# A state-space and spiking feed-forward block: a new order of work at the head, other buffers for the sums of the last two tiles, and a last piece of 224 columns

## The chip, the cores and the metric

The kernel runs on one core of a Trainium2 chip. The core has a matrix engine (TensorE, PE in the profile; its weight loads are listed apart as PEld), a vector engine (VectorE, DVE), an engine for pointwise functions (ScalarE, ACT), GpSimd (POOL) and SyncE (SP), which here only issues the transfers between the device's memory and the core. Each engine works through its own list of instructions in order, and semaphores make it wait for the others. The metric is the device time of one execution in microseconds; of several runs the median is taken.

## The reference

Sixteen sequences of 1024 tokens with 256 features pass two layers, each behind a normalisation whose shift, scale and gate come from a condition vector c:

```python
mod = (_silu(L0_c) @ L0_wmod).reshape(L0_c.shape[0], 6, 1, -1)
sa, ca, ga, sb, cb, gb = (mod[:, 0], ..., mod[:, 5])
ga = (2 * (ga >= 0) - 1) * jnp.maximum(jnp.abs(ga), 0.25)     # gb alike
h = _layernorm(x) * (1 + ca) + sa
x = x + ga * state_space(h)
h = _layernorm(x) * (1 + cb) + sb
x = x + gb * feed_forward(h)
```

The state-space layer computes `Bu = (h @ W_B.T + b_B) * dt`, runs the recurrence `state = A_bar * state + Bu` over the 1024 tokens, with `A_bar = exp(-exp(log_A) * dt)`, and gives `state @ W_C.T + b_C + h @ W_D.T + b_D`. The feed-forward layer squares the positive part of `h @ W_fc.T` (1024 values per token), multiplies by `W_proj.T`, and counts how often a leaky neuron with this input fires in five steps; the count is divided by 5. All of it is in float32.

## The kernel before

**Tiles and stages.** The tokens are cut into 32 tiles of 512, two to a sequence. A tile passes these stages: statistics and normalisation with tokens on the partitions (`moments`, `aggregate`, `root`, `newton_v`, `normalise_by`), a turn to features on the partitions, the product with W_B (`state_input`, tile pb), the bias (`state_bias`), the recurrence (`state_scan`), the two products with W_D and W_C into one sum (`mix_h`, `mix_xs`, tile py), the gated residual (`mix_out`), a turn back, second statistics, a second turn, the expansion (`expand`, tile pf, in four pairs of blocks), its squares (hid), the contraction (`contract`, tile pp, summed over the four pairs), and the neuron (`spike`, line 532). `spike` needs no loop over time: the count is the number of five thresholds that the input exceeds, so it is one compare and four compare-and-adds on DVE, read from the sum. `gated` (ACT) and `output` (POOL and a store, or DVE at the very end) finish a tile.

**Three passes for float32.** Every product is made of halves: a high part that the fast matrix format holds exactly, and the rest, the low part. `PASSES` (line 228) lists (weight half, data half): high with high, low with high, high with low. One 128-row block of 512 columns therefore takes six products. ACT writes a high part (`scaled_hi`, `state_hi`, `S.activation(wb[:, 0], ...)`), DVE the low part (`scaled_lo`, `state_lo`, `halves_lo`, `hidden_lo`).

**Who sets the order.** Nothing is planned by costs: all engines are wrapped in `InOrder` (line 71), so each one executes its instructions in the order in which the program text issues them. What a line waits for is then only data and buffers. The sums lie in three groups of buffers of 512 float32 columns: `ps_f` (four), `ps_y` (two, for the state-space mix) and `ps_p` (two, for the contraction).

**The head, lines 125 to 152 and 604 to 701.** SP issues the loads in text order: cols (c, log_A, biases and log_dt, 20 KB), the first tile xq_0 in two halves, then pieces of `wmod` (wm1), W_B (fb), W_D (fd), W_C (fcm) and so on. `run_idle(n)` issues n products of a zero tile with itself; nothing reads their result. `silu_c` computes SiLU of c: exponentials on ACT, then add, reciprocal and product on DVE. `decay_steps` is a generator of 20 small DVE steps, each dependent on the one before, that gives A_bar; `decay(n)` issues the next n of them, and lines in between use it to fill DVE. `columns(wm, which, name)` computes one 256-wide part of `mod` as columns: eight products 16 columns wide (ps_ca, ps_sa, ps_ga, and ps_cb, ps_sb, ps_gb later). `ps_bb` and `ps_bd`, also 16 wide, carry the shift sa through W_B and W_D. Tiles 0 and 1 are turned on PE (`transpose`, and `transpose_back` into pm); from tile 2 on that goes over memory (`hop`).

Before the change, twelve zero products open the program and two groups of three more stand behind ps_ca and ps_sa. DVE finishes SiLU ahead of the first statistics. The statistics of tile 1 are put between the two scans of tile 0 and behind them (lines 648 and 669).

**The tail, lines 556 to 587 and 956 to 991.** `period_before_last(30)` and `last_tile(31)`. Tile 30's contraction takes the two `ps_p` buffers, which tile 29's spikes read until then. In the last tile the 256 output features are two blocks m of 128: m = 0 is summed over all 512 columns in a `ps_y` buffer, m = 1 in two pieces of 256 columns in the `ps_p` buffers, each piece followed by its spike and its store.

## Time and profile before

| what | value |
|---|---|
| median of 3 runs | 992.76 us (991.89 to 993.47) |
| profiled execution, its own time | 991.63 us |
| its span, first to last instruction | 989.8 us |
| PE busy | 981.9 us, 99% of the span |
| DVE busy | 851.1 us, 86% |
| ACT busy | 767.1 us, 77% |
| POOL busy | 284.5 us, 29% |
| mean granted clock of TensorE | 0.999 |

The page lists an engine's busy time, the chain of work that ended last (followed back from the last instruction to whatever released each step), and groups of alike instructions. Nearly all instructions stand at line 81, the helper that issues in order, so one goes by the tile names: `py<-xsp,wc` is a product that reads xsp and wc and writes py. A row of the chain or of the timeline gives the start in us from the beginning of the span, the duration, the engine and what was done, and, in brackets, how long the engine had been idle and what ended that. In a table of stretches each engine has its busy us and, in brackets, its instructions; the granted clock of TensorE (1.00 is full), the share of the transfer engines and GB/s follow. Rows of one engine can overlap by some 0.1 us, since an instruction begins while the one before it drains.

### The profile page before, as it was taken

How to read it: one execution, taken by the hardware profiler on the slowest of the kernel's cores; microseconds unless marked ns; L12 is line 12 of the kernel's file. 1: busy time of each engine (PE TensorE's matmuls, PEld its weight loads, DVE VectorE, ACT ScalarE, POOL GpSimd, SP SyncE). 2: the span in 40 equal slices, each digit the busy share in tenths (PEclk: the TensorE clock that was granted, in tenths of full speed). 3: DMA queues.
4: the chain of work that ended last, by engine and by line, in shares of the span. 5: the costliest groups of instructions: out<-in, count | busy, mean ns of one | idle time of the engine just before them, and what ended most of it. 6: DMA issues, size and time to landing. Idle time of an engine off the chain costs nothing.

```text
span 989.8 us, 13366 instructions
## 1 busy us (share of the span) xinstructions
PE 981.9 (99%) x4410; PEld 813.8 (82%) x4410; DVE 851.1 (86%) x1618; ACT 767.1 (77%) x1142; POOL 284.5 (29%) x313
## 2 busy tenths in 40 slices
PE   9999999999999999999999999999999999999997
PEld 8888788888888888888888888888888888888886
DVE  8789998888988889888889888889888889887777
ACT  6786887787877887877877877877877878777784
POOL 0002243223233223233133333133332233331122
PEclk9999999999999999999999999999999999999999
DMA  8224555455454455554455454554554554443321
GB/s 312 83 82 153 179 182 149 149 171 168 153 170 137 152 179 153 157 171 133 154 179 158 155 172 127 169 170 152 168 152 146 170 167 153 149 139 128 96 86 43
DMA packets 125350, 150.07 MB, mean 152 GB/s; under 512 B 9568, under 2 KB 89184, under 8 KB 125280
## 3 DMA queue, kind: packets, MB, share of 16 engines
q1 hardware_dynamic: 125280, 149.22, 48.1%
q8 instruction: 34, 0.56, 0.2%
q14 instruction: 36, 0.29, 0.1%
HBM read 85.22 MB, written 63.96 MB: 151 GB/s over the span
## 4 chain that ended last, share of the span: by engine, by line
PE 91%; DVE 5%; ACT 2%; issue 1%; DMA 0%; SPq 0%; DVEq 0%
PE pf L81 33%; PE pp L81 32%; PE py L81 16%; PE pb L81 8%; DVE o L81 2%; PE ps_zero L81 1%; ACT a L81 1%; ACT xn_a L81 1%; ACT hid L81 0%; DMA hop_x<-w_x 0%; DVE h_b L81 0%; DVE st_b L81 0%; DVE x L81 0%; DVE h_a L81 0%; DVE e_b L81 0%
## 5 line engine op out<-in xcount | busy, mean ns | idle before, releaser
L81 PE MATMUL pp<-hid,wp 128*128 128x512 f32 (+1 forms) x1560 | 365.4, 387 | 0.4 <-DVE o L81 0.4
L81 PE MATMUL pf<-h_b,wf 128*128 128x512 f32 x1536 | 363.9, 390 | 0.0
L81 PEld LDWEIGHTS pp<-hid,wp 128*128 128x128 f32 x1560 | 289.2, 188 | 61.4 <-DVE hid L81 1.5
L81 PEld LDWEIGHTS pf<-h_b,wf 128*128 128x128 f32 x1536 | 288.1, 188 | 59.8
L81 ACT ACTIVATE a<-pf,bias_f 128x512 f32<-128x512 f32 x256 | 167.0, 680 | 157.1 <-PE pf L81 157.0
L81 DVE TENSOR_TENSOR hid<-a,hid 128x1024 fp32r<-128x1024 f32 x127 | 152.8, 1223 | 89.2 <-ACT hid L81 89.2
L81 POOL TENSOR_TENSOR o<-o,x 128x512 f32<-128x512 f32 x64 | 110.0, 1739 | 296.0 <-ACT o L81 296.0
L81 DVE SCALAR_TENSOR_TENSOR o<-pp,o 128x512 f32<-128x512 f32 (+1 forms) x260 | 177.5, 683 | 8.0
L81 ACT ACTIVATE hid<-a 128x1024 fp32r<-128x1024 f32 x128 | 135.9, 1061 | 4.0
L81 ACT ACTIVATE a<-a 128x1024 f32<-128x1024 f32 x128 | 135.8, 1061 | 3.9
L81 POOL TENSOR_SCALAR x<-x,gac 128x512 f32<-128x512 f32 x58 | 90.2, 1564 | 51.8 <-DVE o L81 51.8
L81 POOL TENSOR_SCALAR v_a<-mv_a 128x4 f32<-128x4 f32 x26 | 15.6, 600 | 278.0 <-DVE mv_a L81 278.0
L81 PE MATMUL py<-xsp,wc 128*128 128x512 f32 x384 | 92.7, 390 | 0.0
L81 PE MATMUL pb<-h_a,wb 128*128 128x512 f32 x384 | 92.6, 390 | 0.0
L81 PE MATMUL py<-h_a,wd 128*128 128x512 f32 x384 | 92.2, 389 | 0.0
L81 PEld LDWEIGHTS py<-h_a,wd 128*128 128x128 f32 x384 | 72.1, 188 | 14.9
L81 PEld LDWEIGHTS pb<-h_a,wb 128*128 128x128 f32 x384 | 71.9, 188 | 15.0
L81 PEld LDWEIGHTS py<-xsp,wc 128*128 128x128 f32 x384 | 71.8, 188 | 15.0 <-DVE xsp L81 0.3
L81 ACT ACTIVATE xn_a<-xq,m_a,r_a 128x256 f32<-128x256 f32 x123 | 63.8, 592 | 3.2 <-DVE m_a L81 3.2
L81 ACT ACTIVATE xn_b<-xm,m_b,r_b 128x256 f32<-128x256 f32 x120 | 62.0, 588 | 4.0 <-DVE m_b L81 4.0
L81 DVE TENSOR_SCALAR o<-pp 128x512 f32<-128x512 f32 (+1 forms) x65 | 43.4, 668 | 14.1 <-PE pp L81 14.1
L81 ACT ACTIVATE o<-o,gb 128x512 f32<-128x512 f32 x64 | 42.3, 709 | 6.2 <-issue 4.7
(124 smaller groups left out, 835.6 us busy)
## 6 DMA issues: line engine op xcount, KB each, us to landing
x<-in_x SPq DMA_DIRECT2D x32, 512.0 KB, 5.1
out<-o SPq DMA_DIRECT2D x63, 256.0 KB, 6.9
xq<-in_xq SPq DMA_DIRECT2D x31, 512.0 KB, 6.7
hop_a<-w_a SPq DMA_DIRECT2D x120, 128.0 KB, 2.2
v_a<-hop_a SPq DMA_DIRECT2D x30, 512.0 KB, 4.0
hop_x<-w_x SPq DMA_DIRECT2D x120, 128.0 KB, 3.1
xm<-hop_x SPq DMA_DIRECT2D x30, 512.0 KB, 3.2
hop_b<-w_b SPq DMA_DIRECT2D x120, 128.0 KB, 2.2
```

Of the source, the lines that this page charges most:

```text
L81: return self.tc.keep_in_program_order(issue(*args, **kwargs))
```

## The change

In the head:

- SP issues the first half of xq_0, then cols, then the second half.
- The three DVE steps of SiLU move from `silu_c` into the front of `decay_steps` (23 steps now), so they are issued between the first statistics; these come right behind the zero products in the text, and ps_ca behind them. The two groups of three zero products go; the twelve at the start stay.
- The first normalisation gives three of four blocks to DVE. ACT's high part of W_B, s1 and the low part of W_B come behind it; ps_sa comes behind the transposes of a0; the remaining decay steps are spread anew, one behind each low part of h_a0 and six behind both.
- `state_input(0)` is issued in two parts, with ps_bb between them. The low part of W_D moves behind the first scan, and `mix_h(0)` takes its passes in the order high-high, high-low, low-high.
- All four statistics of tile 1 move behind tile 0's scans and the low parts of the states and of W_C. Its normalisation is split S, V, S, V. ps_cb and ps_sb come ahead of the transposes of a1.

In the tail:

- Tile 30's contraction is summed in the `ps_y` buffers. The low part of its first pair of hid is issued ahead of tile 29's second spike.
- In the last tile block m = 0 and the first piece of m = 1 are summed in `ps_p`, the last piece in `ps_y`; the pieces have 288 and 224 columns.

```diff
     col = const.tile([P, KD * NB + 4 * KD + 1], F32, name="col")
-    Q.dma_start(out=col, in_=cols)
     xqs[0] = io.tile([P, SUB, D], F32, tag="xq", name="xq_0", bufs=2)
     for s in (slice(0, 2), slice(2, 4)):
         Q.dma_start(out=xqs[0][:, s], in_=xq[0][:, s])
+        if s.start == 0:
+            Q.dma_start(out=col, in_=cols)
...
-        V.tensor_scalar(sil, sil, 1.0, None, ALU.add)
-        V.reciprocal(sil, sil)
-        V.tensor_tensor(sil, sil, cs, ALU.mult)
     def decay_steps():
+        yield V.tensor_scalar(sil, sil, 1.0, None, ALU.add)
+        yield V.reciprocal(sil, sil)
+        yield V.tensor_tensor(sil, sil, cs, ALU.mult)
...
-    def scaled_lo(key, src):
+    def scaled_lo(key, src, between=lambda: None):
...
+            between()
...
-    def mix_part(t, w, v, first, last):
-        for passes in (PASSES[:2], PASSES[2:]):
+    def mix_part(t, w, v, first, last, order=PASSES):
+        for passes in (order[:2], order[2:]):
...
                 if (t, m) not in accs:
-                    accs[t, m] = ps_p.tile([P, TT], F32, tag="ps_p", name=f"pp_{t}_{m}")
+                    pool, tag = (ps_y, "ps_y") if t == TILES - 2 else (ps_p, "ps_p")
+                    accs[t, m] = pool.tile([P, TT], F32, tag=tag, name=f"pp_{t}_{m}")
...
-        half = TT // 2
+        cut = TT // 2 + 32
...
-        late = [ps_y.tile([P, TT], F32, tag="ps_y", name=f"pp_{t}_0")]
-        late += [ps_p.tile([P, half], F32, tag="ps_p", name=f"pp_{t}_1_{g}") for g in range(2)]
-        for acc, m, cols in zip(late, (0, 1, 1), (slice(0, TT), slice(0, half), slice(half, TT))):
+        for m, cols in ((0, slice(0, TT)), (1, slice(0, cut)), (1, slice(cut, TT))):
             at = m, cols.start
+            pool, tag = (ps_y, "ps_y") if cols.start else (ps_p, "ps_p")
+            acc = pool.tile([P, cols.stop - cols.start], F32, tag=tag, name=f"pp_{t}_{m}_{cols.start}")
...
+    moments("a0", blocks_of(xqs[0]), between=lambda: decay(1))
     ps_ca = columns(wm1, 1, "ca")
-    run_idle(3)
-    ps_sa = columns(wm1, 0, "sa")
-    run_idle(3)
-    decay(3)
-    moments("a0", blocks_of(xqs[0]), between=lambda: decay(1))
     aggregate("a0")
     root("a0")
+    newton_v("a0", lambda: decay(1))
+    normalise_by("a0", blocks_of(xqs[0]), (V, S, V, V))
     S.activation(wb[:, 0], fb, AF.Identity, scale=edt)
-    newton_v("a0", lambda: decay(1))
-    normalise_by("a0", blocks_of(xqs[0]), (V, S, V, S))
+    V.tensor_scalar(s1, ps_ca, 1.0, None, ALU.add)
+    decay(2)
+    V.scalar_tensor_tensor(wb[:, 1], fb, edt, wb[:, 0].bitcast(F32), ALU.mult, ALU.subtract)
+    decay(1)
+    transpose("a0")
+    ps_sa = columns(wm1, 0, "sa")
+    scaled_hi("a0", lambda k: pts["a0", k])
+    scaled_lo("a0", lambda k: pts["a0", k], lambda: decay(1))
     S.activation(sa, ps_sa, AF.Copy)
-    V.tensor_scalar(s1, ps_ca, 1.0, None, ALU.add)
-    V.scalar_tensor_tensor(wb[:, 1], fb, edt, wb[:, 0].bitcast(F32), ALU.mult, ALU.subtract)
-    transpose("a0")
-    decay(5)
+    decay(6)
+    S.activation(wd[:, 0], fd, AF.Copy)
+    S.activation(wc[:, 0], fcm, AF.Copy)
+    state_input(0, (0,))
...
-    scaled_hi("a0", lambda k: pts["a0", k])
-    scaled_lo("a0", lambda k: pts["a0", k])
-    S.activation(wd[:, 0], fd, AF.Copy)
+    state_input(0, (1,))
...
     decay(8)
-    V.tensor_tensor(wd[:, 1], fd, wd[:, 0].bitcast(F32), ALU.subtract)
-    S.activation(wc[:, 0], fcm, AF.Copy)
-    state_input(0)
     state_bias(0)
     state_scan(0, (0,))
-    moments("a1", blocks_of(xqs[1]), blocks=(0, 1))
-    mix_h(0)
+    V.tensor_tensor(wd[:, 1], fd, wd[:, 0].bitcast(F32), ALU.subtract)
+    mix_h(0, (PASSES[0], PASSES[2], PASSES[1]))
...
     state_scan(0, (1,))
-    moments("a1", blocks_of(xqs[1]), blocks=(2, 3))
+    state_hi(0, slice(1, 2))
+    state_lo(0, slice(0, 1))
+    V.tensor_tensor(wc[:, 1], fcm, wc[:, 0].bitcast(F32), ALU.subtract)
+    state_lo(0, slice(1, 2))
+    moments("a1", blocks_of(xqs[1]))
     aggregate("a1")
     root("a1")
-    state_hi(0, slice(1, 2))
-    V.tensor_tensor(wc[:, 1], fcm, wc[:, 0].bitcast(F32), ALU.subtract)
-    state_lo(0, slice(0, 1))
     gates = shift_gate()
     newton_v("a1", lambda: next(gates, None))
-    state_lo(0, slice(1, 2))
     for _ in gates:
         pass
-    normalise_by("a1", blocks_of(xqs[1]), (S, S, V, S))
+    normalise_by("a1", blocks_of(xqs[1]), (S, V, S, V))
     mix_xs(0)
-    transpose("a1")
     ps_cb = columns(wm2, 1, "cb")
     ps_sb = columns(wm2, 0, "sb")
+    transpose("a1")
...
         expand(t, 1)
+        hidden_lo(t, 0)
         spike(t - 1, accs.pop((t - 1, 1)), (1, 0))
-        hidden_lo(t, 0)
```

More of the change, by code (lines that the diff above doesn't have):

```diff
@@ L411, in adaln_kernel, with state_input @@
     pbs = {}
-    def state_input(t):
+    def state_input(t, blocks=range(KD)):
         h = hs[f"a{t}"]
-        for m in range(KD):
+        for m in blocks:
             ps = pbs[t, m] = ps_f.tile([P, TT], F32, tag="ps_f", name=f"pb_{t}_{m}")
@@ L448, in mix_part, with mix_h @@
                          first and passes[0] == PASSES[0], last and passes[0] != PASSES[0], True, passes, True)
-    def mix_h(t):
+    def mix_h(t, order=PASSES):
         for m in range(KD):
             ys[t, m] = ps_y.tile([P, TT], F32, tag="ps_y", name=f"py_{t}_{m}")
-        mix_part(t, wd, hs[f"a{t}"], True, False)
+        mix_part(t, wd, hs[f"a{t}"], True, False, order)
     def mix_xs(t):
```

## The prediction

> **What bounds the kernel now.** I read the page first (busy shares, then the chain that ended last), then that chain in order of time at both ends of the span, then the rows of the vector engine (DVE) and of ScalarE (ACT) for the first 40 us, then a table of stretches for the granted clock. The page says who holds the end:

> ```profile
> span 989.8 us, 13366 instructions
> PE 981.9 (99%) x4410; PEld 813.8 (82%) x4410; DVE 851.1 (86%) x1618; ACT 767.1 (77%) x1142; POOL 284.5 (29%) x313
> ...
> PE 91%; DVE 5%; ACT 2%; issue 1%; DMA 0%; SPq 0%; DVEq 0%
> ```

> TensorE (PE) is the bound nearly everywhere; between 118 and 978 us it runs from one product to the next, and no edit touches that stretch except the last two tiles. So the change is decided at its two ends. The chain in order of time, at the head:

> ```profile
> 1.47 4.47 PE ps_zero L81 x12
> 5.93 0.92 PE ps_ca L81 x8
> 6.85 0.79 PE ps_zero L81 x3
> 7.64 0.80 PE ps_sa L81 x8
> 8.44 0.80 PE ps_zero L81 x3
> 9.24 0.87 PE pt_a L81 x8
> 10.11 0.80 PE ps_bb L81 x8
> 10.91 2.92 PE pb L81 x12
> ...
> 23.78 0.92 PE pm L81 x8
> 24.70 2.77 PE pb L81 x12
> ...
> 39.27 0.02 issue
> 39.30 0.02 ACT sil L81
> ```

> PE holds the head without a gap up to 39.3 us, the two groups of three zero products among its work; then ACT and DVE hold the chain until 118. A head that ends later or earlier on PE at 39.3 moves everything behind it by as much. What DVE does meanwhile:

> ```profile
> 14.57 0.73 DVE L81 BATCH_NORM_STATS2 st_a<-xq 128x6 f32<-128x256 f32 x2
> ...
> 21.92 1.36 DVE L81 TENSOR_TENSOR x<-x,x 128x512 f32<-128x512 f32 x2 [0.96 <-ACT x L81]
> ```

> Here the reader is to see how near DVE is to the bound: tile 1's statistics lie between the scans, and the two adds that PE's transposes pm wait for come 0.96 us after DVE ran out of work. The tail, from the same chain:

> ```profile
> 950.29 8.39 PE pp L81 x36
> 958.68 5.44 PE pf L81 x24
> ...
> 978.10 0.70 DVE o L81
> ...
> 986.14 0.48 DVE o L81
> ```

> 36 products at the steady 2.72 us per 12 are 8.16; tile 30's first sums take 8.39, so 0.23 us are waits. From 978.1 DVE holds the end.

> **The change part by part: the head.** All times are in the profiled execution's span. A row's mean overlaps the next row by some 0.08 us, so I add the distances between starts.

> Loads: the first half of xq_0 goes from second to first place on SP's queue, cols from first to second. Before, they were issued at 0.72 (cols) and 1.15 and landed 1.8 and 2.6 us later, at 2.5 and 3.75. The half issued at 0.72 lands at 3.3; cols, issued at 1.2 behind it, between 3.0 (its own 1.8) and 3.75 (the 2.6 of the row before it); I take 3.15. The second half landed at 4.5 and has the same bytes ahead of it: 4.25 to 4.5. Nothing behind them moves, and the weights of ps_ca land at 5.7 as before.

> First statistics: four BATCH_NORM_STATS2 with one step after each were 4.02 to 5.61. Now they start at 3.3, the steps between them are SiLU's (its reciprocal 0.35, the rest 0.1 each), and the third waits for the second half: aggregates end at 5.7 (5.98 before). Root and Newton take 1.33 as before: m_a at 7.03. ACT's wb no longer lies before its xn block. DVE now does three of the four blocks, 3 x 0.33 from 7.06: xn complete at 8.13 (8.43 before, with PE taking it only at 9.08). So PE idles from 6.8 to about 8.2, the six zero products (1.59 us of chain) shrink to this gap, and the transposes end at 8.95 instead of 10.11.

> PE then does ps_sa (0.9), the six products of pb's block 0 from 9.6 (1.4, with DVE's second low part, 10.0 to 10.75, just in time), ps_bb until 12.0, block 1 until 13.4. At pb PE is 1.16 ahead.

> DVE does not keep that lead. Behind the second low part (start 10.0) come seven dependent steps of the decay, 0.19 each, until 12.0, when ps_bb is ready too; two bias_b (0.20 each), four more steps (0.75): scan 0 starts at 13.2, against 13.44. From there I add DVE's own distances in the new order: scan 1.13, wd low 0.61, scan 1.13, xsp low 0.60, wc low 0.58, xsp low 0.60, four statistics 1.29, aggregates 0.36, ACT's root with its two handovers 0.36, Newton with four gate steps 1.16: m_a at 21.0, against 19.6. The statistics, which lay in the shade of the scans, and wd low are now in this row of work. ACT's two blocks of xn, 1.03 with the handover, and its first x, 0.80, follow; then the two adds 0.66 and 0.69, and the last four transposes of pm 0.42. That is 13.2 + 11.42: tile 1's pb starts at 24.62 instead of 24.46, **0.16 later**. PE is not short of other work before that: mix_h ends at 16.1 (its low weights are ready at 15.0, and the new order wants them last), mix_xs at 20.7, ps_cb, ps_sb and the transposes of a1 at 23.3; then it waits for the adds. ACT's scaled_hi of a1 stays behind its x and in front of pb. So the lead of 1.16 is gone at pm, where a wait for DVE stands in place of the zero products.

> Later in the head: DVE starts tile 0's second statistics 0.9 later (after the low part of h_a1), the root 0.5 later, and xn_b is complete at 30.2 where PE wants it at 30.2. No further loss. load_q(2) waits for xn_a0 and leaves 0.3 earlier, load_q(3) for xn_a1 and load(2) for the adds, each 0.9 later; xq_3 is read at 49, x_2 at 37. They cost nothing as long as they land in the 6 to 7 us of their rows.

> **The tail.** Tile 30's sums take the two buffers that tile 31's mix left at 929.7, so PE no longer waits for tile 29's second spike (950.85), and the low part of hid 30,0, now ahead of that spike, is ready at 948.5 instead of 951.98. Both waits go: **-0.23**. The spike ends 1.1 later, at 952; its gating on ACT comes at 956.9. The last tile's sums go where tile 29's and tile 30's first spikes have long released. DVE's row from 966 to 978 starts with PE's end of tile 30, so it moves with it; the 0.3 that PE waits for tile 31's low parts stays.

> The last pieces: from 512 and 256 columns DVE's distance is 0.725 and 0.459, so 288 costs 0.492, 224 costs 0.425. Five each: the sum over both pieces is the same, and both start when DVE is free (PE ends the 224 piece 0.3 before). Only the final operation on 224 columns saves 0.03, its store of 112 KB perhaps 0.04: **-0.07**.

> Sum: 989.8 + 0.16 - 0.23 - 0.07 = 989.66, and 1.83 around the span as in the profiled execution (991.63): 991.5. That execution lies 1.13 under the median of 992.76, which gives 992.6 by medians. One thing speaks for somewhat less: before, PE has no slack from 1.47 to 9.24, so any delay of the cold first products reaches the end, and the runs differ by 1.84 us (991.63 to 993.47) for a reason that this trace does not show; the new gap of 1.4 us at 6.8 would swallow such a delay. At nothing to half of the 1.13, I take 0.3: **992.3**.

> [...] Granted clock first. The twelve cold zero products took 4.47 us where twelve of pf take 2.88, so a cold spell costs 1.6. In a stretch with only narrow products and transposes the clock stayed full:

> ```profile
> 21.05:24.45 3.40, 3.40 (x33) 3.40 (x32) 2.53 (x5) 2.84 (x6) 0.00 (x0) 1.00 0.59 188
> ```

> By that row, narrow work is enough, and the price of removing the zero products is nothing. [...] I go by the row, which has no idle time in it, though; that difference is a rival.

> **The rivals.** (1) Slower, by the clock: without zero products PE has no 512-column work from 5.93 to 9.6 and idles 1.4 of that. If the clock falls there, pb and the first mix run cold: 1.6, or 3.2 if the spell is twice as long, so 994 to 995.6. It is slower than 0.2% (2 us) from about ten to twelve cold products on. Against it: the row above. Chance 0.15. (2) Faster: DVE's row is shorter than I add, and PE keeps its 1.16: 992.76 - 1.16 - 0.30 = 991.3; with a delay of the first products also swallowed, down to 990.2. It needs DVE to make 1.3 us less between 13.2 and 23.5, and DVE's rows there have no idle time to lose. Chance 0.22. (3) The tail's 0.23 stays, because the product waits for something else than the spike and hid: 992.6, inside my forecast. The forecast (0.63, own range 991.6 to 993.2) takes the landings of xq_0 and cols from 0.1 early to 0.3 late, and 0.3 on DVE's row.

> **How the numbers follow.** 0.2% is about 2 us, what a measurement of this kernel can tell from no change: under 990.8 or over 994.75. Half of rival 2 lies under 990.8, with a little of the forecast: 0.13. Of rival 1, some two thirds lie over 994.75 when both spells count and the median is hit: 0.10. The rest, 0.77, is within. The range 990.4 to 994.5 leaves out about one in ten on each side.

> **What the next profile would show.** Right: ps_ca followed by a gap of some 1.4 us on PE; pb of tile 0 near 9.6; scan 0 near 13.2; pm waiting for DVE x, and tile 1's pb at 24.6; tile 30's first 36 pp in 8.16; pieces of 288 and 224 with DVE last. Wrong: a granted clock under 1.00 or 512-column products 0.4 apart after 6 us (rival 1); pm following the transposes of a1 without a wait (rival 2); a wait of pp for hid or o at 950 (rival 3). A second wait on PE between 25 and 39, where I found room of 0.1 to 0.3 only (xn_b), would make it slower than I say.

## The result and the profile after

The changed kernel takes 995.78 us (median of 17 runs, 991.92 to 998.49) against 992.62 us for the kernel before (17 runs, 991.75 to 993.47): ratio 1.0024, interval 1.0015 to 1.0033. It is slower by 0.24% (the ratio is taken over all runs; between the medians the difference is 3.2 us, 0.32%), and its runs form two groups: six of 991.9 to 992.8 us whose mean granted clock is 0.998 or 0.999, and eleven of 994.7 to 998.5 us with a clock of 0.992 to 0.997. Below, a run with 0.997 or less is said to have fallen. Two executions far outside all others, 1094.32 us of e5 and 2022.04 us of the kernel before in the same comparison, are left out of the figures. The profiled execution is one of the second group (997.29 us). From its page, the span, the busy times and the granted clock in 40 slices:

```profile
span 995.5 us, 13352 instructions
PE 986.3 (99%) x4404; PEld 817.9 (82%) x4404; DVE 852.0 (86%) x1620; ACT 766.1 (77%) x1140; POOL 284.6 (29%) x313
...
PEclk7999999999999999999999999999999999999999
```

Six products fewer, and PE is busy 4.4 us longer. The clock is low in the first slice only. The chain in order of time, at the head:

```profile
1.62 4.36 DMA xq<-in_xq
...
9.20 1.32 PE pt_a L81 x8
10.52 1.39 PE ps_sa L81 x8
11.91 2.75 PE pb L81 x6
14.65 1.52 PE ps_bb L81 x8
16.18 2.75 PE pb L81 x6
18.92 3.68 PE py L81 x12
...
30.62 2.85 PE pb L81 x12
```

Six products of pb take 2.75 us; in the kernel before twelve took 2.92. Tile 1's pb starts at 30.62, against 24.70 before. A table of stretches (busy us of PE, PEld, DVE, ACT and POOL with their instructions, then TensorE's granted clock) shows why:

```profile
7.12:10.53 3.41, 2.23 (x19) 1.98 (x18) 2.97 (x19) 1.92 (x4) 0.00 (x0) 1.00 1.03 385
10.53:13.95 3.42, 3.42 (x13) 3.02 (x13) 2.81 (x12) 2.09 (x5) 0.00 (x0) 0.50 1.03 420
13.95:17.36 3.41, 3.41 (x13) 3.03 (x12) 1.04 (x6) 0.69 (x1) 0.00 (x0) 0.50 1.02 420
17.36:20.77 3.41, 3.41 (x9) 2.64 (x8) 2.91 (x4) 1.21 (x2) 0.00 (x0) 0.50 1.04 386
20.77:24.20 3.43, 3.43 (x25) 3.07 (x23) 3.43 (x12) 0.64 (x1) 0.00 (x0) 1.00 0.13 42
```

The clock is halved from 10.53 to 20.77 us, three times 3.41 us; in e9, below, it is halved once for as long (10.79 to 14.20). Stretches of this length, counted from where the clock became full, are called steps here. In the step before the fall (7.12 to 10.53) PE was busy 2.23 us, with ps_ca, the transposes and nothing 512 columns wide. This is the first rival of the prediction. The tail, from the chain, and the row of DVE that begins the last piece, from the timeline:

```profile
955.99 8.16 PE pp L81 x36
964.15 5.44 PE pf L81 x24
```

```profile
989.77 0.39 DVE L81 TENSOR_SCALAR o<-pp 128x224 f32<-128x224 f32 x1 [0.28 <-issue]
```

Tile 30's first 36 products take 8.16, so the two waits there are gone, as predicted. Ahead of the piece of 224 columns DVE stands still for 0.28 us for nothing that the profile shows.

### The profile page after: what moved, and what is told of

The parts are those of the page before. It is cut to its first block, busy times and chain, and to the rows that moved or that the text cites. A ratio compares the mean times of both kernels' runs of the same rounds, so it can differ in the third digit from the quotient of the medians.

```text
span 995.5 us, 13352 instructions
## 1 busy us (share of the span) xinstructions
PE 986.3 (99%) x4404; PEld 817.9 (82%) x4404; DVE 852.0 (86%) x1620; ACT 766.1 (77%) x1140; POOL 284.6 (29%) x313
## 4 chain that ended last, share of the span: by engine, by line
PE 90%; DVE 5%; ACT 2%; DMA 1%; issue 1%; SPq 0%; DVEq 0%
PE pf L81 33%; PE pp L81 32%; PE py L81 16%; PE pb L81 8%; DVE o L81 2%; ACT a L81 1%; ACT xn_a L81 0%; DMA xq<-in_xq 0%; ACT hid L81 0%; DMA hop_x<-w_x 0%; DVE h_b L81 0%; DVE st_b L81 0%; DVE x L81 0%; DVE h_a L81 0%; DVE w_x L81 0%
## 5 line engine op out<-in xcount | busy, mean ns | idle before, releaser
L81 PE MATMUL pp<-hid,wp 128*128 128x512 f32 (+2 forms) x1560 | 365.1, 386 | 0.4 <-DVE o L81 0.4
L81 PE MATMUL pf<-h_b,wf 128*128 128x512 f32 x1536 | 363.9, 390 | 0.0
L81 PEld LDWEIGHTS pp<-hid,wp 128*128 128x128 f32 x1560 | 289.5, 188 | 60.6 <-DVE hid L81 1.2
L81 PEld LDWEIGHTS pf<-h_b,wf 128*128 128x128 f32 x1536 | 288.2, 188 | 59.7
L81 ACT ACTIVATE a<-pf,bias_f 128x512 f32<-128x512 f32 x256 | 167.0, 680 | 156.5 <-PE pf L81 156.4
L81 DVE TENSOR_TENSOR hid<-a,hid 128x1024 fp32r<-128x1024 f32 x127 | 152.8, 1223 | 88.4 <-ACT hid L81 88.4
L81 POOL TENSOR_TENSOR o<-o,x 128x512 f32<-128x512 f32 x64 | 110.1, 1741 | 295.4 <-ACT o L81 295.4
L81 DVE SCALAR_TENSOR_TENSOR o<-pp,o 128x512 f32<-128x512 f32 (+1 forms) x260 | 177.5, 683 | 8.0
L81 ACT ACTIVATE hid<-a 128x1024 fp32r<-128x1024 f32 x128 | 135.9, 1062 | 4.0
L81 ACT ACTIVATE a<-a 128x1024 f32<-128x1024 f32 x128 | 135.8, 1061 | 3.9
L81 POOL TENSOR_SCALAR x<-x,gac 128x512 f32<-128x512 f32 x58 | 90.2, 1565 | 51.5 <-DVE o L81 51.5
L81 PE MATMUL pb<-h_a,wb 128*128 128x512 f32 x384 | 95.4, 398 | 0.0
L81 POOL TENSOR_SCALAR v_a<-mv_a 128x4 f32<-128x4 f32 x26 | 15.6, 600 | 278.4 <-DVE mv_a L81 278.4
L81 PE MATMUL py<-h_a,wd 128*128 128x512 f32 x384 | 93.3, 392 | 0.0
L81 PE MATMUL py<-xsp,wc 128*128 128x512 f32 x384 | 92.6, 390 | 0.0
L81 PEld LDWEIGHTS pb<-h_a,wb 128*128 128x128 f32 x384 | 73.5, 192 | 15.3
L81 PEld LDWEIGHTS py<-h_a,wd 128*128 128x128 f32 x384 | 73.0, 190 | 15.3
L81 PEld LDWEIGHTS py<-xsp,wc 128*128 128x128 f32 x384 | 71.9, 188 | 14.8
L81 ACT ACTIVATE xn_a<-xq,m_a,r_a 128x256 f32<-128x256 f32 x121 | 62.8, 593 | 3.7 <-DVE m_a L81 3.7
L81 ACT ACTIVATE xn_b<-xm,m_b,r_b 128x256 f32<-128x256 f32 x120 | 62.0, 588 | 3.5 <-DVE m_b L81 3.5
L81 DVE TENSOR_SCALAR o<-pp 128x512 f32<-128x512 f32 (+1 forms) x65 | 43.5, 669 | 14.7 <-PE pp L81 14.3
L81 ACT ACTIVATE o<-o,gb 128x512 f32<-128x512 f32 x64 | 42.4, 711 | 6.4 <-issue 4.7
```

What stands on the lines that cost most here:

```text
L81: return self.tc.keep_in_program_order(issue(*args, **kwargs))
```

## The experiments

**Is it the clock? (e1)** Six wide zero products go back into the gap:

```diff
     ps_ca = columns(wm1, 1, "ca")
+    run_idle(6)
```

> The changed kernel with six zero products of 512 columns put back behind ps_ca, into the gap before the transposes of tile 0; nothing else is undone. Clock theory (the changed kernel loses its time because TensorE's clock falls to half after a stretch without wide products): the clock stays full in every run (mean granted clock 0.998 or more), the median is 992.0 to 992.8, and the spread shrinks from 6.6 us to under 2. Order theory (DVE's longer row and the waits at pm, or the later landing of xq_0, cost the time): the zero products change nothing, median 995 to 996.

Measured: 993.29 us (992.55 to 993.64, 11 runs) against 992.61 before, ratio 1.0006 (0.9997 to 1.0015). All eleven runs at 0.998 or 0.999. From the PE timeline of its profile:

```profile
7.04 1.63 PE L81 MATMUL ps_zero<-zero 128*128 128x512 f32 x6
8.50 1.04 PE L81 MATMUL pt_a<-ident,xn_a 128*128 128x128 f32 x8
...
10.19 1.70 PE L81 MATMUL pb<-h_a,wb 128*128 128x512 f32 x6
...
24.42 1.32 PE L81 MATMUL pm<-ident,x 128*128 128x128 f32 x8 [0.20 <-DVE x L81]
25.49 3.00 PE L81 MATMUL pb<-h_a,wb 128*128 128x512 f32 x12
```

Work that is thrown away makes the kernel 2.5 us faster, because pb runs at full clock (1.70 for six). So the clock is the greater part of the 3.2 us. The median is a little above what I expected: by medians 0.7 us over the kernel before remain at full clock, though the interval of the ratio reaches 1, and the row of pm shows a wait for DVE.

**Is it idle time, or the lack of wide products? (e2, e9, e3)** e2 fills the gap with narrow products:

```diff
+    def run_narrow(n):
+        for _ in range(n):
+            PE.matmul(ps_zero[:, 0:NB], lhsT=zero[:, 0:P], rhs=zero[:, 0:NB], start=True, stop=True)
...
     ps_ca = columns(wm1, 1, "ca")
+    run_narrow(12)
```

> The changed kernel with twelve products of 16 columns of the zero tile behind ps_ca: the gap is filled as long as in the run with wide zero products (12 x 0.11 us), but with narrow work. If what makes the clock fall is idle time of TensorE, the clock stays full as with the wide ones: median 992.0 to 992.8, all clocks 0.998 or more. If what counts is wide work, narrow products count for little: median 994.5 to 996, more than half of the runs with a clock of 0.997 or less.

Measured: 1002.62 us (999.32 to 1003.98, 5 runs), all clocks 0.995 or less. The run was sized wrongly: a float32 product of this form is recorded as two instructions (ps_ca, too, is four products and eight instructions), and the 24 of them took 4.87 us (0.20 each, against 0.13 in e9 at full clock, so most ran at half clock) and held up the transposes until 12.3. That explains the length; the fall of the clock needs the next run, with `run_narrow(4)`:

> The changed kernel with four products of 16 columns of the zero tile behind ps_ca. Twelve of them were recorded as 24 instructions and took 4.9 us, three times the gap; four are eight instructions, like ps_ca itself, and take 0.9 us, so they fill the gap without holding up the transposes. If idle time makes the clock fall: full clock in all runs, median 992.4 to 993.3. If narrow work does not count: most runs fall, median 994.5 to 997, as without any fill (995.8).

Measured: 996.71 us (995.27 to 998.79, 4 runs) against 993.25, ratio 1.0042 (1.0026 to 1.0059); all four runs fell. Its PE timeline and a table of stretches:

```profile
7.95 1.04 PE L81 MATMUL ps_zero<-zero 128*128 128x16 f32 x8
9.12 1.32 PE L81 MATMUL pt_a<-ident,xn_a 128*128 128x128 f32 x8
10.27 1.25 PE L81 MATMUL ps_sa<-sil,wm 128*128 128x16 f32 x8
11.37 2.91 PE L81 MATMUL pb<-h_a,wb 128*128 128x512 f32 x6
```

```profile
7.38:10.79 3.41, 3.29 (x28) 3.04 (x28) 3.14 (x18) 2.11 (x5) 0.00 (x0) 1.00 1.06 396
10.79:14.20 3.41, 3.41 (x12) 2.83 (x12) 2.49 (x10) 1.75 (x4) 0.00 (x0) 0.50 1.02 412
...
24.44:27.85 3.41, 3.19 (x27) 2.71 (x27) 2.63 (x8) 3.41 (x7) 0.00 (x0) 1.00 0.39 138
```

PE is busy 3.29 of 3.41 us, and the clock falls from 1.00 to 0.50. It is not idle time. Nor is it the lack of wide products alone: in the last row no product of 512 columns starts either, and PE idles longer, but 15 transposes start instead of eight, and the clock stays full. The counterpart is the order of the kernel before without its two groups of zero products (e3):

```diff
     ps_ca = columns(wm1, 1, "ca")
-    run_idle(3)
     ps_sa = columns(wm1, 0, "sa")
-    run_idle(3)
```

> The kernel before without its two groups of three zero products; its order is kept. TensorE then has no wide product from ps_ca to pb, some 3.9 us, but idles only about 1.1 us of that in two pieces. If the missing zero products alone make the clock fall, it falls here too: median 994 to 996 with a spread of several us. If it takes the gap that the new order has, the clock stays full: median 992.0 to 992.8 (the transposes begin at 8.5 instead of 9.1, which DVE's row gives back in part).

Measured: 994.85 us (990.89 to 997.29, 11 runs) against 992.61, ratio 1.0015 (1.0005 to 1.0026). Eight of the eleven runs fell (0.994 to 0.997, 993.4 to 997.3 us); the three at full clock took 990.89, 991.58 and 992.74. The profiled execution stayed at full clock:

```profile
7.42 1.06 PE L81 MATMUL ps_sa<-sil,wm 128*128 128x16 f32 x8 [0.24 <-DMA wm<-in_wmod]
8.34 1.07 PE L81 MATMUL pt_a<-ident,xn_a 128*128 128x128 f32 x8
9.24 0.96 PE L81 MATMUL ps_bb<-sa,fb 128*128 128x16 f32 x8
10.05 3.06 PE L81 MATMUL pb<-h_a,wb 128*128 128x512 f32 x12
...
23.74 3.00 PE L81 MATMUL pb<-h_a,wb 128*128 128x512 f32 x12
```

The old order loses its clock too once the zero products are gone, with hardly a gap. They are what keeps it. At full clock the old order without them looks like the fastest head (median 991.58, and tile 1's pb at 23.74), but three runs that spread over 1.9 us don't show it.

**How many are enough? (e8, e6)** e8 is e1 with `run_idle(3)`:

> The changed kernel with three zero products behind ps_ca instead of six. If 0.7 us of wide products in the stretch are enough: every run at full clock and a median of 992.4 to 993.2 (up to 0.7 under the run with six, as far as its zero products hold up the transposes). If the clock needs more, some runs fall by 2 to 5 us and the median is over 993.5.

Measured: 993.57 us (992.97 to 996.73, 12 runs) against 992.94, ratio 1.0007 (0.9994 to 1.0020). Nine runs at full clock (992.97 to 993.91), three fell (994.97 to 996.73). Three are not always enough here; in the same comparison four of 34 runs of the kernel before fell too. e6 is the kernel before with the tail's edits and without the second group:

```diff
     ps_ca = columns(wm1, 1, "ca")
     run_idle(3)
     ps_sa = columns(wm1, 0, "sa")
-    run_idle(3)
```

> The kernel before with the tail's edits and only the first group of three zero products (behind ps_ca); the second group, behind ps_sa, is gone. The kernel before without both groups reached 990.9 to 992.7 where the clock stayed full and lost about 3 us where it fell (8 of 11 runs). If 0.7 us of wide products in the stretch are enough for the clock: median 991.2 to 991.7, all clocks 0.998 or more, better than both kernels. If not: a spread of several us and a median over 993.

Measured: 991.82 us (991.17 to 995.80, 12 runs) against 992.94, ratio 0.9989 (0.9977 to 1.0000); one run in twelve fell. It was the fastest in its comparison, by 1.1 us, though the interval reaches 1, and more than half of that may be the tail's (see e4).

**The tail by itself (e4).** The three edits of the tail on the kernel before:

> The kernel before with the edits of the tail alone (tile 30's sums in the state-space buffers, the low part of hid 30,0 ahead of the spike, a last piece of 224 columns). By the prediction -0.30 us. By the profile of the changed kernel, where DVE's work from the end of the sum of 512 columns takes 8.78 us instead of 8.53, the last piece costs 0.25 and the buffers give 0.23: no difference, 992.5 to 992.7.

Measured: 991.98 us (991.37 to 992.67, 11 runs) against 992.61, ratio 0.9992 (0.9983 to 1.0001): -0.63 us, with an interval that holds both -0.30 and nothing. There is no gap ahead of the last piece:

```profile
984.50 0.38 DVE L81 TENSOR_SCALAR o<-pp 128x224 f32<-128x224 f32 x1
984.92 1.67 DVE L81 SCALAR_TENSOR_TENSOR o<-pp,o 128x224 f32<-128x224 f32 x4
986.62 0.45 DVE L81 SCALAR_TENSOR_TENSOR o<-o,gb,x 128x224 f32<-128x224 f32 x1
```

From the end of the sum of 512 columns to the last operation DVE takes 8.41 us (978.66 to 987.07); before it was 8.53, in the changed kernel 8.78.

**What costs at full clock? (e5, e7)** e1 with the loads in the old order:

```diff
     col = const.tile([P, KD * NB + 4 * KD + 1], F32, name="col")
+    Q.dma_start(out=col, in_=cols)
...
-        if s.start == 0:
-            Q.dma_start(out=col, in_=cols)
```

> The changed kernel with the six zero products behind ps_ca (full clock), and the loads in the order of the kernel before: cols, then the two halves of xq_0. In profiles so far the second half landed 4.4, 3.2 and 4.2 us after its issue where cols lies between the halves, and 2.9, 3.2 and 3.3 where cols comes first. If the load order does that and it counts, the median falls from 993.3 to 992.6 to 993.0. If the landing only scatters, or DVE has room for it, it stays at 993.3 (+-0.3).

Measured: 993.61 us (992.97 to 994.32, 11 runs, all at full clock) against 992.94, ratio 1.0004 (0.9993 to 1.0014): by medians the same 0.7 over the kernel before as e1. The load order makes no difference that shows; the landing of the second half (4.4 us after its issue in the changed kernel's profile, 3.2 to 3.5 in e1, e7 and e8) scatters.

e7 is e1 with tile 1's statistics back between the scans:

```diff
     state_scan(0, (0,))
+    moments("a1", blocks_of(xqs[1]), blocks=(0, 1))
     V.tensor_tensor(wd[:, 1], fd, wd[:, 0].bitcast(F32), ALU.subtract)
...
     state_scan(0, (1,))
+    moments("a1", blocks_of(xqs[1]), blocks=(2, 3))
+    aggregate("a1")
+    root("a1")
     state_hi(0, slice(1, 2))
...
     state_lo(0, slice(1, 2))
-    moments("a1", blocks_of(xqs[1]))
-    aggregate("a1")
-    root("a1")
```

> The changed kernel with the six zero products behind ps_ca, and tile 1's statistics back where the kernel before has them: two between the scans, two behind, with the aggregates and the root ahead of the states' low parts. By the prediction's sum (DVE's row decides when pm can start) pm follows the transposes of a1 without a wait, tile 1's pb starts 0.4 to 0.6 earlier, and the median falls from 993.3 to 992.7 to 992.9. If PE's own row decides, nothing changes: 993.3 (+-0.3).

Measured: 994.05 us (992.67 to 998.55, 12 runs) against 992.94, ratio 1.0014 (0.9998 to 1.0029); the eight runs with a clock of 0.998 or more have a median of 993.8. From its PE timeline:

```profile
16.67 1.19 PE L81 MATMUL py<-h_a,wd 128*128 128x512 f32 x4 [0.51 <-DVE wd L81]
...
23.99 1.07 PE L81 MATMUL pt_a<-ident,xn_a 128*128 128x128 f32 x8
24.90 1.04 PE L81 MATMUL pm<-ident,x 128*128 128x128 f32 x8
25.70 3.08 PE L81 MATMUL pb<-h_a,wb 128*128 128x512 f32 x12
```

A miss: pm now follows without a wait, but two statistics ahead of wd's low part make PE wait 0.51 us for that instead. Tile 1's pb comes 17.3 us after the first transpose, in e1 17.0. In both places of the statistics PE waits for DVE once on this way, for the adds or for wd. Four of these runs fell by the clock (0.994 to 0.996) in spite of the six zero products; why, when none of e1 and e5 did, was not found.

**The gap ahead of the last piece (e10).** The tail on the old head, and two instructions more on DVE:

```diff
-    V.memset(eps, EPS)
+    for _ in range(3):
+        V.memset(eps, EPS)
```

> The kernel before with the edits of the tail, and two more instructions on DVE in the first microsecond (eps is set three times instead of once). In the five profiles with the new head DVE stands still for 0.25 to 0.28 us ahead of the piece of 224 columns, for nothing that the profile shows, and a load of instructions follows 0.7 us later; with the old head there is no such gap, and the load follows 1.7 us later. DVE has 1620 instructions with the new head, 1618 with the old one. If the place in DVE's list makes the gap, it appears here, and the load moves 0.9 us forward. If the gap comes from something else in the new head, it does not appear.

Measured: 992.52 us, a single run. The gap does not appear. The load of instructions moved, but to 1.5 us ahead of the piece instead of 0.7 behind it. So in this run the load came elsewhere with two instructions more in the list; that its place makes the gap is not shown, and the gap's cause stays open. It stands in the profiles of the changed kernel and of e1, e2, e5, e7, e8 and e9, all with the new head, at 0.25 to 0.28 us; with the same tail on the old head (e4, e6, e10) it does not.

## Why the prediction was wrong

**The step that failed** is "narrow work is enough, and the price of removing the zero products is nothing". e1 shows the price: 2.5 us of the 3.2. I read it from a row that held more than narrow work. The 21.05 to 24.45 stretch of the kernel before holds 16 transposes, twice as many as the new order has from ps_ca to pb, 16 narrow products and the last 0.17 us of a wide one. Nor is it one of the clock's steps in that execution, which are these:

```profile
18.25:21.67 3.42, 3.42 (x18) 2.72 (x19) 2.63 (x14) 2.06 (x5) 0.00 (x0) 1.00 0.85 299
21.67:25.08 3.41, 3.41 (x31) 3.32 (x30) 3.16 (x7) 2.22 (x5) 0.00 (x0) 1.00 0.69 226
```

In the first start 11 wide products and 6 transposes, in the second 3 wide ones, 10 transposes and 16 narrow ones. In the records the granted clock keeps a value for a multiple of 3.41 us (983.04 us, 288 times, at 1.00 in the kernel before; once at 1.00, then three times at 0.50 in the head of the changed kernel; once at 0.50 in e9), and the first of these steps starts at another time in each execution (the clock became full at 4.38 us in e6, 4.60 in the kernel before, 5.55 in e3, 5.59 in e1, 7.12 in the changed kernel and 7.38 in e9). So I go by what lies in a step; no run shows by itself that this is what counts. Sorted by the products that start in it: the step before the fall has no wide product, 8 transposes and 9 narrow ones in the changed kernel, and no wide one, 8 transposes and 19 narrow ones in e9. Steps that kept the clock have 2 wide products with 6 transposes (e3), 2 with 8 (e6), 1 with 14 (e7), none with 15 (e6 from 21.44, e9 from 24.44). By these steps wide products and transposes seem to count, products of 16 columns hardly; one step with 5 wide products, no transpose and 13 narrow ones fell (e2). By time, from start to start in the timelines, the steps that lost the clock hold 1.15 us (changed kernel, e9) and 1.32 us (e2) of wide products and transposes, and those that kept it at least 1.29 (e3), then 1.55 (e6 from 4.38). So I estimate a limit near 1.3 us of such work per step, from these few steps alone. In the new order the stretch from ps_ca to pb (6.86 to 11.75 in the profile) is longer than a step and holds only the 8 transposes, so by this estimate whether a run falls depends on where the steps lie; eleven in seventeen did, of which one was profiled.

**The rival was priced right and given too little.** "1.6, or 3.2 if the spell is twice as long": the changed kernel's runs at full clock have a median of 992.35, the others of 995.97, 3.6 apart. The spell in the profile lasts three steps: in the first two the wide products were mixed with ps_sa and ps_bb, 5 and 4 wide ones to a step, and the clock was full again behind the third, with 8. I gave this 0.15 against a row cut where I liked. Of the two things that the rival names, the idle time is not needed: the longest gap ahead of a fall in the head was 1.18 us (changed kernel), and e9 fell with 0.12 us idle in the step. Nor does the lack of wide products decide alone: 15 transposes kept the clock without one (e6, e9).

**The head at full clock.** "The transposes end at 8.95": in e1 they begin at 8.50 and end by 9.4, 0.4 later. The second half of xq_0 landed 3.2 us after its issue, at 4.8, where I took 4.25 to 4.5, and xn is complete at 8.50 instead of 8.13; the zero products that e1 adds end at about the same time, so the two can't be told apart. "pb from 9.6": 10.19. "Scan 0 starts at 13.2": 13.99, as much later. "11.42" from there to tile 1's pb: 11.50, with pm waiting for DVE's adds as predicted. So the sum of DVE's row was right, and its start was missed by 0.8. "0.16 later" is then about 1 us: e1 lies 1.3 over e4, which has the same tail on the old head, and 0.26 of that is the gap ahead of the last piece. Single profiles scatter too much to confirm it: tile 1's pb starts at 24.46 in the kernel before, 25.36 in e4 and 25.49 in e1. For the changed kernel itself this must be read with care, since no profile of it at full clock is at hand; its six runs at full clock (median 992.35) lie below e1, perhaps because no zero products held up the transposes. That they lie on the forecast of 992.3 is in part luck: they are a selection, and the terms of the sum did not come out one by one.

**The tail.** The 0.23 of the buffers came as predicted (8.39 to 8.16 in the chain), so rival 3 is out. The last piece saves 0.12 on the old head instead of 0.07, and on the new head it is overdrawn by a gap that I did not foresee. Together e4 measured -0.63 with an interval of about 0.9 to either side, which does not tell -0.30 from it.

**The gap that swallows delays.** "I take 0.3" off for it: not settled. The runs of the changed kernel at full clock spread over 0.9 us where those of the kernel before spread over 1.7, but they are a selection. One source of such delays is in the profiles: the twelve first zero products took 4.36 us in e6 (clock full at 4.38), 4.47 in the kernel before (4.60), 4.92 in e3 and e1 (5.55 and 5.59) and 5.49 in the changed kernel and e9 (7.12 and 7.38), the longer the later the clock became full.

**Rival 2** (PE keeps its lead of 1.16) is out by its sign: in e1, e5 and e8 pm waits 0.2 us for DVE behind the transposes of a1. The way from the first transpose of tile 0 to tile 1's pb is 17.0 us there, and 15.4 in the kernel before and in e4; 0.8 of the difference is ps_sa, which the new order puts behind the transposes.

## What to carry to other kernels

Products whose result nobody reads can be load-bearing: before taking them away, count what remains in any stretch as long as the clock's step (3.41 us here), by time and kind, and don't trust a stretch whose limits you chose yourself. When runs of one kernel fall into two groups, read the granted clock of each before looking at the order of its work. A lead won on one engine is worth only what the next engine can take: here 1.2 us on PE ended at a row of DVE work, and the one other order that was tried (e7) brought nothing.
